# Selective-scan kernel: scans of places 1 and 2 over 513 columns, with hand-drawn waits on three PSUM banks

## The chip, the cores and the metric

The kernel runs on one core of one Trainium2 chip. The time is that of the device, in microseconds (us), from the start of the program on the core to its end; a result is the median of several executions. Five engines work side by side, each through its own queue in order: PE (matrix multiply), DVE (vector), ACT (scalar, with the activation functions), POOL (a second, slower vector engine) and SP (here it only issues DMAs). An instruction that waits holds up everything behind it on its engine.

## What is computed

A batch of 4 images of 128 channels and 128 x 128 points goes through two layers. The first, cut to what matters here, is a selective scan along the 16384 points of each image, for 256 inner channels with 16 states each:

```
delta = softplus(dt @ dt_proj_w.T + dt_proj_b)
A = -exp(A_log)
def step(h, inp):
    d_t, B_t, C_t, u_t = inp
    dA = exp(d_t[:, :, None] * A)
    h = h * dA + d_t[:, :, None] * B_t[:, None, :] * u_t[:, :, None]
    y = einsum('bds,bs->bd', h, C_t)
    return (h, y)
```

Around the scan stand small matrix products (an MLP, a projection, a convolution of 4 taps), a gate with silu(z), an output projection and a group norm. The second layer (group norm, an aggregation with softmax weights, and a filter in the Fourier domain) comes after it, partly between the chunks of later images.

## The kernel before, in words

**Chunks and units.** `block0` (from L148) cuts each image into 32 chunks of T = 512 points, 128 chunks k in all, and works on a chunk as 8 **units** U0 to U7 (u = 0..7: channel half j = u // 4, state group r = u % 4). A unit has 4 **places** p = 0..3; a place is 128 partitions (32 channels x 4 states) by 512 points. So a unit has four scans, one per place.

**One scan** is a `tensor_tensor_scan` on DVE (L412): state = da * state + b along the 512 points, where `da` = exp(delta * A) comes from ACT (L393) and b = du * B. It starts from the state that the same place had at the end of the chunk before: a column of a small tile `st`, given as an operand with one value per partition. Only in the first chunk of an image (k % 32 == 0) is the start the constant 0.0. For places 1 to 3, b is made by POOL in tile `hb` (L363, function `dbu`); for place 0 it is made by four PE transposes into the PSUM bank `b0` (L383, `dbu_turn`, here called the **turn**). `da` of place 0 lies in SBUF, those of places 1, 2 and 3 in one PSUM bank each.

**After a scan** the state is multiplied by C. For places 2 and 3 DVE does it (L414; the scan wrote in place over `da`), and ACT copies the last column to `st` (L415). For places 0 and 1 the scan writes to SBUF (`h`) and POOL multiplies both in one instruction of 1024 columns (L419); ACT copies the two last columns in the next slot (the **late** copy, printed under L554, the line that runs it). `by_vector` (L345) moves single places between the two: in odd chunks place 1 of U6 is multiplied by DVE too; in the chunks that also do the first group norm of the image before (k >= 32 and 2 <= k % 32 < 18, 48 chunks, here **norm chunks**) place 2 of U6 is done by POOL. `sums` (L422) adds the four products of a unit into the bank `y` with PE (L433); for U0 and U4 the bank is new, and a product with `diag` (L429) comes first, which must wait until the DVE gate (L443) has read the bank's old content.

**Order of the work.** Nothing is scheduled automatically: a list `todo` gives each piece a slot and a phase (L539 to L554), and the order in which pieces are emitted is the order on each engine. Each unit has an even slot (scans of places 0 and 1) and an odd slot (scans of places 2 and 3). Within a slot the phases run in the order of L551: turn, sums, pe, exps, late, act, pool, dbu, early, gate, scans, dve, end. What matters of it on ACT, before the change:

- even slot: `da` of places 2 and 3 of this unit, then the slot's other work (phases act and pool)
- odd slot: `da` of place 1 of the next unit, the late copy, the slot's other work, `da` of place 0 of the unit after the next (phase early), then the two copies of L415, which wait for the products on DVE

The other work of the 16 slots of a chunk: U1's even slot has silu of z and u (L242, L239), U3's has softplus (L275), each with two loads of an activation table around it; U3's odd slot copies `xdt` (L286); U4's and U5's odd slots start with, or contain, scalings `bt` of a transposed du (L304), which need PE transposes `pt_dut` (L293, `du_turn`) emitted in the pe phase of slots 8 and 11. Slot 11 is U5's odd slot. The gate of one half runs in slot 2 (U1), that of the other in slot 10 (U5). In 42 chunks (k % 32 >= 18 from k = 50 on, here **aggregation chunks**) the second layer's aggregation (L663, L667) and some transforms run in between too. The other 38 chunks that are not norm chunks are called plain.

Buffers: `hb` has 4, `h` 3, each PSUM bank of `b0` and `da` one. Which engine may touch a PSUM bank when is settled by the framework's waits, tile by tile.

Of the kernel before, what the change touches and what calls it, by code (L numbers as in the profile page):

```python
# [26 lines left out]
F32 = mybir.dt.float32  # L27
AF = mybir.ActivationFunctionType
ALU = mybir.AluOpType
# [4 lines left out]
P = 128  # L34
T = 512
DG = 32
SQ = 4
NP = 16
# [8 lines left out]
def kernel(ctx: ExitStack, tc: tile.TileContext, a: dict, out: bass.AP):  # L47
# [101 lines left out]
    spec = [dpool.tile([H, C, 2, WF], F32, tag=f"spec_{b}", name=f"spec_{b}") for b in range(EARLY)]  # L149
    shared = SimpleNamespace(**{k: v for k, v in locals().items() if k not in ("ctx", "tc")})  # L150
    block0(tc, shared)
    block1(tc, shared)


def block0(tc, s):
    nc, B, NCH, NH, NS, NG, ND, R, NX, KC, HALO, C, L, NF, DI = (
        s.nc, s.B, s.NCH, s.NH, s.NS, s.NG, s.ND, s.R, s.NX, s.KC, s.HALO, s.C, s.L, s.NF, s.DI,
    )
    NT = T // P
    with ExitStack() as ctx:  # L160
        def pool(name, bufs, **kw):
            return ctx.enter_context(tc.tile_pool(name=name, bufs=bufs, **kw))

        p1 = pool("p1", 1)
        p2 = pool("p2", 2)
        hpool = pool("hb", 4)
        tiny = pool("tiny", 2)
# [5 lines left out]
        psd = pool("psd", 1, space=PSUM)  # L173
# [4 lines left out]
        def turn_bank(n):  # L178
            return pst.tile([P, T], F32, tag="pt", name=f"pt_{n}")

        st = {}
        stats, outs = s.stats, s.outs

# [154 lines left out]
        def norming(k):  # L338

            return k >= NCH and 2 <= k % NCH < 2 + NCH // 2  # L340

        def place(r, p):


            return (p - r) % ND  # L345

        def by_vector(k, j, r, p):

            if norming(k):
                return p > 1 and (j, r, p) != (1, 2, 2)  # L350
            return p > 1 or (k % 2 == 1 and (j, r, p) == (1, 2, 1))

        def dbu(u):

            k, r = divmod(u, NH * NG)
            j, r = divmod(r, NG)
            d = st[k]
            hb = d["hb", j, r] = hpool.tile([P, ND, T], F32, tag="hb", name=f"hb_{k}_{j}_{r}")
            p = 1
            while p < NG:  # L360
                m = place(r, p)
                n = min(NG - p, ND - m)
                nc.gpsimd.tensor_tensor(  # L363
                    hb[:, p : p + n, :], d["du", j][:, m : m + n, :], d["B"][:, p - 1 : p - 1 + n, :], ALU.mult
                )
                p += n

        def pair(n):

            k, r = divmod(n, NP)  # L370
            u, p = divmod(r, ND // 2)
            j, r = divmod(u, NG)
            return k, j, r, 2 * p

        def dbu_turn(n):

            k, j, r, p = pair(n)
            d = st[k]
            if p == 0:
                b = d["b0"] = psd.tile([P, T], F32, tag="b0", name=f"b0_{k}_{j}_{r}")  # L380
                for t in range(NT):
                    src = d["bt"][:, t, j * ND + place(r, 0), :, :].rearrange("p s d -> p (s d)")
                    nc.tensor.transpose(b[:, t * P : (t + 1) * P], src, s.ident)  # L383

        def exps(n, qs):

            k, j, r, p = pair(n)
            d = st[k]
            for q in qs:
                m = place(r, p + q)  # L390
                c = (j * NG + p + q) * ND + m
                da = (psd if p + q else p2).tile([P, T], F32, tag=f"da{p + q}", name=f"da{p + q}_{k}_{j}_{r}")
                nc.scalar.activation(da, d["delta", j][:, m, :], AF.Exp, scale=s.amat[:, c : c + 1])  # L393
                d["da", j, r, p + q] = da

        def scans(n):


            k, j, r, p = pair(n)
            d = st[k]  # L400
            hb = d["hb", j, r]
            das = [d.pop(("da", j, r, p + q)) for q in range(2)]
            dve = [q for q in range(2) if by_vector(k, j, r, p + q)]
            pool = [q for q in range(2) if q not in dve]
            last = d["last", j, r, p] = tiny.tile([P, 2], F32, tag=f"st{j}_{r}_{p}", name=f"st_{k}_{j}_{r}_{p}")
            if pool:
                h = p2.tile([P, 2, T], F32, tag="h", name=f"h_{k}_{j}_{r}_{p}", bufs=3)
            for q in range(2):
                b = hb[:, p + q, :] if p + q else d.pop("b0")
                init = 0.0 if k % NCH == 0 else st[k - 1]["last", j, r, p][:, q : q + 1]  # L410
                o = das[q] if q in dve else h[:, q, :]
                nc.vector.tensor_tensor_scan(o, das[q], b, init, ALU.mult, ALU.add)  # L412
            for q in dve:
                nc.vector.tensor_tensor(hb[:, p + q, :], das[q], d["C"][:, p + q, :], ALU.mult)  # L414
                nc.scalar.copy(last[:, q : q + 1], das[q][:, T - 1 : T])  # L415
            if pool:
                q = slice(pool[0], pool[-1] + 1)
                ps = slice(p + pool[0], p + pool[-1] + 1)
                nc.gpsimd.tensor_tensor(hb[:, ps, :], h[:, q, :], d["C"][:, ps, :], ALU.mult)  # L419
                todo[n + 1, "late"].append(partial(nc.scalar.copy, last[:, q], h[:, q, T - 1]))  # L420

        def sums(u):  # L422

            k, r = divmod(u, NH * NG)
            j, r = divmod(r, NG)
            d = st[k]
            if r == 0:
                y = d["y", j] = psy.tile([P, T], F32, tag="y", name=f"y_{k}_{j}")
                nc.tensor.matmul(y, s.diag[:, j, :], d["u"][:, j, :], start=True, stop=False)  # L429
            y = d["y", j]  # L430
            for p in range(ND):
                m = place(r, p)
                nc.tensor.matmul(  # L433
                    y[m * DG : (m + 1) * DG, :], s.sel, d["hb", j, r][:, p, :], start=False, stop=r == NG - 1
                )

        def post(k):
# [66 lines left out]
        n_chunks = B * NCH  # L504
        todo = defaultdict(list)
# [33 lines left out]
        for n in range(n_chunks * NP):  # L539
            if n % 2 == 0:  # L540
                todo[n - 3, "early"].append(partial(exps, n, (0,)))
            todo[n - 1, "exps"].append(partial(exps, n, (1,) if n % 2 == 0 else (0, 1)))
            todo[n - 1, "turn"].append(partial(dbu_turn, n))
            todo[n, "scans"].append(partial(scans, n))
            if n % 2 == 0:
                todo[n - 2, "dbu"].append(partial(dbu, n // 2))
            else:
                todo[n + 2, "sums"].append(partial(sums, n // 2))
        slots = [n for n, _ in todo]
        with tc.manual_schedule():  # L550
            for n in range(min(slots), max(slots) + 1):  # L551
                for phase in ("turn", "sums", "pe", "exps", "late", "act", "pool", "dbu", "early", "gate", "scans", "dve", "end"):
                    for f in todo[n, phase]:
                        f()  # L554

# [500 lines left out]
```

## Time and profile before

| | us |
|---|---|
| median of 3 runs | 7172.46 (7171.05 to 7173.44) |
| the profiled execution, its own time | 7175.45 |
| its span | 7173.6 |
| main part with the scans (first to last scan) | 48.7 to 6407.5 |
| scans L412, place 0 and 1 to SBUF: x992, x1000 | 1258.3, 1251.6 |
| scans L412 in place, x1976 | 2419.8 |
| products L414 on DVE, x2040 | 1296.1 |
| products L419 on POOL, x1072 | 2435.0 |
| du * B on POOL, L363, x1536 | 3605.7 |
| exponentials on ACT, L393, x4096 | 2794.1 |

The times of the rows are sums over the whole span. Engines overlap, so the rows don't add up to the span: what counts is which engine has no idle time in a stage, and what a late result holds up there.

### The profile page before, as it was taken

What the parts mean: (1) busy time and instruction counts of PE and PEld (TensorE: products, weight loads), DVE (VectorE), ACT (ScalarE), POOL (GpSimd) and SP (SyncE); (2) the same over time, 40 slices, a digit from 0 to 9 for tenths busy, and PEclk for the clock granted to TensorE, in tenths of its full rate; (3) what the DMA queues carried; (4) which work ended last, traced back from release to release, by engine and by line L of the source; (5) the groups of instructions that cost most, each with busy time, mean ns of one, the idle gap of its engine ahead of it and who ended that gap; (6) DMA issues with size and microseconds to landing.
All of it is one profiled execution on the core that took longest, in us unless ns stands there. A gap on an engine that the chain in (4) does not pass through costs nothing.

```text
span 7173.6 us, 91384 instructions
## 1 busy us (share of the span) xinstructions
PE 5904.2 (82%) x26708; PEld 2626.8 (37%) x26708; DVE 6892.9 (96%) x7966; ACT 6143.9 (86%) x13658; POOL 6892.5 (96%) x3188
## 2 busy tenths in 40 slices
PE   6888888788787788888888788888887888867998
PEld 2333333233222233333333333333333333326888
DVE  6999999999999999999999999999999999989777
ACT  6888888888888888888888888898888888878876
POOL 6999999999999999999999999999999999988887
PEclk8888888888888889998989899999898899979999
DMA  5666666666777777777777777777777777769866
GB/s 139 160 160 152 163 159 151 165 159 165 191 176 192 179 171 176 172 184 175 189 196 186 188 176 175 178 177 184 189 191 194 177 179 177 172 164 306 236 185 162
DMA packets 905480, 1286.20 MB, mean 179 GB/s; under 512 B 81672, under 2 KB 356752, under 8 KB 904976
## 3 DMA queue, kind: packets, MB, share of 16 engines
q1 hardware_dynamic: 904832, 1280.09, 71.9%
q8 instruction: 210, 3.44, 0.2%
q14 instruction: 294, 2.41, 0.1%
q10 hardware_dynamic: 144, 0.26, 0.0%
HBM read 1023.45 MB, written 256.58 MB: 178 GB/s over the span
## 4 chain that ended last, share of the span: by engine, by line
DVE 41%; ACT 29%; issue 11%; PE 10%; DMA 5%; POOL 3%; SPq 1%; DVEq 0%; ACTq 0%; POOLq 0%
DVE da L412 20%; DVE h L412 12%; ACT da L393 12%; DVE hb L414 5%; ACT L393 3%; DMA rdelta<-dd 2%; ACT L275 2%; ACT delta L275 2%; ACT bt L304 2%; POOL hb L363 2%; DVE zs L443 1%; PE y L433 1%; POOL hb L419 1%; ACT L242 1%; DMA xt<-x 1%
## 5 line engine op out<-in xcount | busy, mean ns | idle before, releaser
L363 POOL TENSOR_TENSOR hb<-rdu,rB 128x1536 f32<-128x1536 f32 (+2 forms) x1536 | 3605.7, 2364 | 22.4 <-DMA rdelta<-dd 21.3
L393 ACT ACTIVATE da<-rdelta,amat 128x512 f32<-128x512 f32 x4096 | 2794.1, 700 | 138.3 <-DVE h L412 133.9
L419 POOL TENSOR_TENSOR hb<-h,rC 128x1024 f32<-128x1024 f32 (+1 forms) x1072 | 2435.0, 2274 | 88.8 <-DVE h L412 73.4
L412 DVE TENSOR_TENSOR_SCAN da<-da,st,hb 128x512 f32<-128x512 f32 x1976 | 2419.8, 1267 | 21.5 <-ACT da L393 14.3
L433 PE MATMUL y<-hb,sel 128*32 128x512 f32 x8192 | 1313.4, 717 | 2.9 <-POOL hb L419 2.7
L414 DVE TENSOR_TENSOR hb<-da,rC 128x512 f32<-128x512 f32 x2040 | 1296.1, 674 | 3.0
L412 DVE TENSOR_TENSOR_SCAN h<-da,st,b 128x512 f32<-128x512 f32 x992 | 1258.3, 1268 | 1.7 <-PE b L383 1.6
L412 DVE TENSOR_TENSOR_SCAN h<-da,st,hb 128x512 f32<-128x512 f32 x1000 | 1251.6, 1255 | 1.8 <-ACT da L393 1.8
L383 PE MATMUL b<-ident,bt 128*128 128x128 f32 x4096 | 748.4, 305 | 516.1 <-DVE h L412 390.6
L234 PE MATMUL pp_cv<-xm,wck 128*128 128x512 f32 x2048 | 1014.3, 640 | 1.6 <-ACT xm L217 0.8
L304 ACT ACTIVATE bt<-pt_dut,xdt 128x256 f32<-128x256 f32 x2048 | 839.4, 474 | 184.5 <-PE pt_dut L293 184.3
L383 PEld LDWEIGHTS b<-ident,bt 128*128 128x128 f32 x4096 | 531.3, 154 | 1017.1 <-DVE h L412 692.8
L415 ACT COPY st<-da 128x1 f32<-128x1 f32 x2040 | 273.1, 160 | 474.2 <-DVE hb L414 471.1
L234 PEld LDWEIGHTS pp_cv<-xm,wck 128*128 128x128 f32 x2048 | 395.9, 204 | 651.0 <-issue 422.1
L828 POOL TENSOR_TENSOR wb<-wb,term 128x1040 f32<-128x1040 f32 x192 | 461.0, 2401 | 70.8 <-ACT term L822 62.9
L293 PE MATMUL pt_dut<-ident,du 128*128 128x128 f32 x1024 | 232.4, 338 | 285.1 <-ACT xdt L286 174.9
L429 PE MATMUL y<-u,diag 128*128 128x512 f32 x512 | 303.0, 675 | 188.7 <-DVE zs L443 187.3
L293 PEld LDWEIGHTS pt_dut<-ident,du 128*128 128x128 f32 x1024 | 132.2, 162 | 604.8 <-POOL du L312 475.9
L393 ACT ACT_TABLE_LOAD x262 | 336.1, 1283 | 12.1 <-DMA rdelta<-dd 7.4
L312 POOL TENSOR_TENSOR du<-delta,u 128x512 f32<-128x512 f32 x256 | 318.8, 1267 | 25.8 <-ACT delta L275 25.8
L223 PE MATMUL pp_z<-xm,win 128*128 128x512 f32 x512 | 274.5, 634 | 51.8 <-ACT fq L497 46.2
L267 PE MATMUL pp_dt<-xd,wdt 8*128 8x512 f32 x512 | 284.8, 642 | 33.0 <-ACT pp_o L457 23.5
(160 smaller groups left out, 8139.8 us busy)
## 6 DMA issues: line engine op xcount, KB each, us to landing
rdelta<-dd SPq DMA_DIRECT2D x1024, 256.0 KB, 4.7
rdu<-dd SPq DMA_DIRECT2D x1024, 256.0 KB, 7.5
rC<-bc SPq DMA_DIRECT2D x512, 256.0 KB, 7.3
rB<-bc SPq DMA_DIRECT2D x512, 192.0 KB, 4.7
dd<-delta SPq DMA_DIRECT2D x256, 256.0 KB, 7.2
dd<-du SPq DMA_DIRECT2D x256, 256.0 KB, 5.7
ft<-in_filt_w SPq DMA_DIRECT2D x104, 520.0 KB, 7.0
ob<-o SPq DMA_DIRECT2D x128, 256.0 KB, 2.1
```

Of the source, the lines that this page charges most:

```text
L234: nc.tensor.matmul(ps["cv", j], w, d["xm"][:, t : t + T], start=t == 0, stop=t == KC - 1)
L293: nc.tensor.transpose(ps["dut"][:, 2 * t + j, :], d["du"][:, j, at : at + P], s.ident)
L304: nc.scalar.activation(d["bt"][:, 2 * h + t, :, q, :], src, AF.Copy, scale=d["xdt"][:, 2 * h + t, R + q : R + q + 1])
L312: nc.gpsimd.tensor_tensor(du, d["delta"][:, j, :], d["u"][:, j, :], ALU.mult)
L363: nc.gpsimd.tensor_tensor(hb[:, p : p + n, :], d["du", j][:, m : m + n, :], d["B"][:, p - 1 : p - 1 + n, :], ALU.mult)
L383: nc.tensor.transpose(b[:, t * P : (t + 1) * P], src, s.ident)
L393: nc.scalar.activation(da, d["delta", j][:, m, :], AF.Exp, scale=s.amat[:, c : c + 1])
L412: nc.vector.tensor_tensor_scan(o, das[q], b, init, ALU.mult, ALU.add)
L414: nc.vector.tensor_tensor(hb[:, p + q, :], das[q], d["C"][:, p + q, :], ALU.mult)
L419: nc.gpsimd.tensor_tensor(hb[:, ps, :], h[:, q, :], d["C"][:, ps, :], ALU.mult)
L433: nc.tensor.matmul(y[m * DG : (m + 1) * DG, :], s.sel, d["hb", j, r][:, p, :], start=False, stop=r == NG - 1)
L828: nc.gpsimd.tensor_tensor(wb, wb, u[n].terms[f], ALU.add)
```

## The change

The PSUM banks of `b0`, `da` 1 and `da` 2 become one tile `band` of three banks side by side. For a unit whose place 1 is multiplied by POOL (all but U6 of chunks that are not norm chunks), the scans of places 1 and 2 take 513 columns: the first is the last column of the bank to the left, with the constant start 0.0, and `hb` has a column more, whose value for places 1 and 2 is the old state. So 0.0 * a + b gives the old state, and the scan goes on from there. The old state gets there by an ACT copy of two columns (`carry`; in the first chunk of an image by a POOL memset). As the scans now read or write the last column of the neighbouring bank, the kernel draws the waits on the three banks itself (`on_band`): each user waits for the last users of its banks on the other engines, and no wait is drawn between users of different banks.

With it go: DVE multiplies place 1 of U6 in every chunk that is no norm chunk (before: odd ones); the order in an odd slot is place 3, then 2, for scans, products and copies, and ACT makes `da` 3 before `da` 2; `da` 1 of the next unit is emitted inside `scans` of the odd slot, after the scan of place 2 and so behind the early `da` 0; the turn comes after sums; and `hb` and `h` have rows of 513 columns, of which the products and sums use the last 512.

```diff
+        band = psd.tile([P, 3 * T], F32, tag="band", name="band")
+        users = []
+        def on_band(engine, banks, made):
+            i = made.ins
+            seen = set()
+            for e, b, j in reversed(users):
+                if e == engine:
+                    continue
+                if not b & banks:
+                    tc.declare_no_dep(i, j, reason="another bank")
+                    continue
+                for bank in b & banks:
+                    if (e, bank) not in seen:
+                        seen.add((e, bank))
+                        tc.add_manual_dep(
+                            i, j.name, mybir.DependencyInfo(mybir.DependencyClass.Sync, mybir.DependencyReason.DATA),
+                            reason="same bank",
+                        )
+            users.append((engine, banks, i))
+            del users[:-40]
...
-            return p > 1 or (k % 2 == 1 and (j, r, p) == (1, 2, 1))
+            return p > 1 or (j, r, p) == (1, 2, 1)
...
-            hb = d["hb", j, r] = hpool.tile([P, ND, T], F32, tag="hb", name=f"hb_{k}_{j}_{r}")
+            hb = d["hb", j, r] = hpool.tile([P, ND, 1 + T], F32, tag="hb", name=f"hb_{k}_{j}_{r}")
...
+        def carried(k, j, r):
+            return () if by_vector(k, j, r, 1) else (1, 2)
+        def carry(u):
+            k, r = divmod(u, NH * NG)
+            j, r = divmod(r, NG)
+            if carried(k, j, r):
+                o = st[k]["hb", j, r][:, 1:3, 0]
+                if k % NCH == 0:
+                    nc.gpsimd.memset(o, 0.0)
+                else:
+                    nc.scalar.copy(o, st[k - 1]["last", j, r][:, 1:3])
...
+                if p + q in (1, 2):
+                    da = band[:, (p + q) * T : (p + q + 1) * T]
...
-                h = p2.tile([P, 2, T], F32, tag="h", name=f"h_{k}_{j}_{r}_{p}", bufs=3)
+                h = p2.tile([P, 2, 1 + T], F32, tag="h", name=f"h_{k}_{j}_{r}_{p}", bufs=3)
+            order = (1, 0) if p else (0, 1)
+            for q in order:
+                if p + q in carried(k, j, r):
+                    a = band[:, (p + q) * T - 1 : (p + q + 1) * T]
+                    o = a if q in dve else h[:, q, :]
+                    made = nc.vector.tensor_tensor_scan(o, a, hb[:, p + q, :], 0.0, ALU.mult, ALU.add)
+                    on_band("DVE", {p + q - 1, p + q}, made)
+                    continue
...
+            if p and n + 1 < n_chunks * NP:
+                exps(n + 1, (1,))
+            for q in [q for q in order if q in dve]:
...
-            todo[n - 1, "exps"].append(partial(exps, n, (1,) if n % 2 == 0 else (0, 1)))
+            if n % 2 or n == 0:
+                todo[n - 1, "exps"].append(partial(exps, n, (1, 0) if n % 2 else (1,)))
...
+                todo[n - 1, "carry"].append(partial(carry, n // 2))
...
-                for phase in ("turn", "sums", "pe", "exps", "late", "act", "pool", "dbu", "early", "gate", "scans", "dve", "end"):
+                for phase in ("sums", "turn", "pe", "exps", "late", "carry", "act", "pool", "dbu", "early", "gate", "scans", "dve", "end"):
```

More of the change, by code (lines that the diff above doesn't have):

```diff
@@ L363, in dbu @@
                 nc.gpsimd.tensor_tensor(
-                    hb[:, p : p + n, :], d["du", j][:, m : m + n, :], d["B"][:, p - 1 : p - 1 + n, :], ALU.mult
+                    hb[:, p : p + n, 1:], d["du", j][:, m : m + n, :], d["B"][:, p - 1 : p - 1 + n, :], ALU.mult
                 )
                 p += n
+        def carried(k, j, r):
[9 more added lines that the diff above has]
+                    nc.scalar.copy(o, st[k - 1]["last", j, r][:, 1:3])
         def pair(n):
@@ L379, in dbu_turn @@
             if p == 0:
-                b = d["b0"] = psd.tile([P, T], F32, tag="b0", name=f"b0_{k}_{j}_{r}")
+                b = band[:, 0:T]
                 for t in range(NT):
                     src = d["bt"][:, t, j * ND + place(r, 0), :, :].rearrange("p s d -> p (s d)")
-                    nc.tensor.transpose(b[:, t * P : (t + 1) * P], src, s.ident)
+                    on_band("PE", {0}, nc.tensor.transpose(b[:, t * P : (t + 1) * P], src, s.ident))
         def exps(n, qs):
@@ L391, in exps @@
                 c = (j * NG + p + q) * ND + m
-                da = (psd if p + q else p2).tile([P, T], F32, tag=f"da{p + q}", name=f"da{p + q}_{k}_{j}_{r}")
-                nc.scalar.activation(da, d["delta", j][:, m, :], AF.Exp, scale=s.amat[:, c : c + 1])
+                if p + q in (1, 2):
+                    da = band[:, (p + q) * T : (p + q + 1) * T]
+                else:
+                    da = (psd if p else p2).tile([P, T], F32, tag=f"da{p + q}", name=f"da{p + q}_{k}_{j}_{r}")
+                made = nc.scalar.activation(da, d["delta", j][:, m, :], AF.Exp, scale=s.amat[:, c : c + 1])
+                if p + q in (1, 2):
+                    on_band("ACT", {p + q}, made)
                 d["da", j, r, p + q] = da
@@ L404, in scans @@
             pool = [q for q in range(2) if q not in dve]
-            last = d["last", j, r, p] = tiny.tile([P, 2], F32, tag=f"st{j}_{r}_{p}", name=f"st_{k}_{j}_{r}_{p}")
+            if p == 0:
+                d["last", j, r] = tiny.tile([P, ND], F32, tag=f"st{j}_{r}", name=f"st_{k}_{j}_{r}")
+            last = d["last", j, r][:, p : p + 2]
             if pool:
-                h = p2.tile([P, 2, T], F32, tag="h", name=f"h_{k}_{j}_{r}_{p}", bufs=3)
[L408 to L412, printed above, removed]
@@ L413, in scans @@
-            for q in dve:
-                nc.vector.tensor_tensor(hb[:, p + q, :], das[q], d["C"][:, p + q, :], ALU.mult)
-                nc.scalar.copy(last[:, q : q + 1], das[q][:, T - 1 : T])
+                h = p2.tile([P, 2, 1 + T], F32, tag="h", name=f"h_{k}_{j}_{r}_{p}", bufs=3)
[7 more added lines that the diff above has]
+                    continue
+                b = hb[:, p + q, 1:] if p + q else band[:, 0:T]
+                init = 0.0 if k % NCH == 0 else st[k - 1]["last", j, r][:, p + q : p + q + 1]
+                o = das[q] if q in dve else h[:, q, 1:]
+                made = nc.vector.tensor_tensor_scan(o, das[q], b, init, ALU.mult, ALU.add)
+                if p + q < 3:
+                    on_band("DVE", {p + q}, made)
@@ new lines, in scans @@
+            if p and n + 1 < n_chunks * NP:
+                exps(n + 1, (1,))
+            for q in [q for q in order if q in dve]:
+                made = [
+                    ("DVE", nc.vector.tensor_tensor(hb[:, p + q, 1:], das[q], d["C"][:, p + q, :], ALU.mult)),
+                    ("ACT", nc.scalar.copy(last[:, q : q + 1], das[q][:, T - 1 : T])),
+                ]
+                if p + q < 3:
+                    for engine, i in made:
+                        on_band(engine, {p + q}, i)
@@ L418, in scans @@
                 ps = slice(p + pool[0], p + pool[-1] + 1)
-                nc.gpsimd.tensor_tensor(hb[:, ps, :], h[:, q, :], d["C"][:, ps, :], ALU.mult)
-                todo[n + 1, "late"].append(partial(nc.scalar.copy, last[:, q], h[:, q, T - 1]))
+                nc.gpsimd.tensor_tensor(hb[:, ps, 1:], h[:, q, 1:], d["C"][:, ps, :], ALU.mult)
+                todo[n + 1, "late"].append(partial(nc.scalar.copy, last[:, q], h[:, q, T]))
         def sums(u):
@@ L433, in sums @@
                 nc.tensor.matmul(
-                    y[m * DG : (m + 1) * DG, :], s.sel, d["hb", j, r][:, p, :], start=False, stop=r == NG - 1
+                    y[m * DG : (m + 1) * DG, :], s.sel, d["hb", j, r][:, p, 1:], start=False, stop=r == NG - 1
                 )
```

## The prediction

> **What bounds the kernel now.** I read the page's busy shares first, then stretches of one chunk each, then the groups kept apart by form, then the order of time on single engines. The shares leave DVE and POOL level:
>
> ```profile
> PE 5904.2 (82%) x26708; PEld 2626.8 (37%) x26708; DVE 6892.9 (96%) x7966; ACT 6143.9 (86%) x13658; POOL 6892.5 (96%) x3188
> ```
>
> The stretches are an even plain chunk, an odd one and a norm chunk (busy us of PE, PEld, DVE, ACT, POOL):
>
> ```profile
> 458.25:506.62 48.37, 40.45 (x157) 15.10 (x156) 48.37 (x51) 41.70 (x93) 47.50 (x22) 0.90 0.67 159
> 506.62:555.73 49.11, 38.49 (x150) 13.80 (x150) 49.08 (x52) 42.02 (x94) 49.11 (x24) 0.87 0.66 157
> 1978.49:2028.78 50.29, 40.20 (x156) 14.60 (x155) 50.26 (x54) 43.23 (x95) 50.06 (x24) 0.92 0.75 184
> ```
>
> DVE has no idle time in any of them: it is the bound. POOL has 0.87 us of slack in two plain chunks together, 0.23 in a norm chunk. ACT idles 7 us a chunk, but its queue is in order, so what counts is when each exponential lands.
>
> **What the constant start saves.** Rows by form:
>
> ```profile
> L412 DVE TENSOR_TENSOR_SCAN da<-da,st,hb 128x512 f32<-128x512 f32 x1976 | 2419.8, 1267 | 21.5 <-ACT da L393 14.3 <-POOL hb L363 3.6 <-issue 3.4
> ...
> L412 DVE TENSOR_TENSOR_SCAN da<-da,hb 128x512 f32<-128x512 f32 x64 | 74.5, 1209 | 1.4 <-issue 1.4
> ...
> L412 DVE TENSOR_TENSOR_SCAN h<-da,hb 128x512 f32<-128x512 f32 x32 | 38.3, 1197 | 3.8 <-POOL hb L363 3.5 <-ACT da L393 0.2
> ```
>
> With a column as start a scan takes 1.267 (1.255 to SBUF, place 1), from the constant 1.209 and 1.197. Starts show the same step: 1.174 becomes 1.114, 60 ns. The 513th column costs at most 1.2 us / 512 = 2 ns, so 58 ns a scan, on DVE, the bound. A plain chunk has 7 such units, 14 scans, 0.81 us; a norm chunk 16 scans, 0.93. Bounds: crossing a bank edge is in no row; the saving could be nothing.
>
> **What it moves.** U6's place 1 on DVE in every plain chunk: the odd chunk is 0.74 longer than the even one, so the mean 48.74 becomes 49.11 - 0.81 = 48.30 before new waits. POOL gives up one 512-column product (2363 - 1276 ns = 1.09 us) in even chunks: (47.50 + 49.11 - 1.09) / 2 = 47.8, so DVE stays the bound. A norm chunk: DVE 50.29 - 0.93 = 49.36; POOL's 50.06 becomes its floor, 0.23 won at most. Rows of 513 columns on POOL: L899 writes 8 rows apart, 520 columns in 1298 ns, where the line through 512 (1276) and 1024 columns (2363) gives 1293, so I take 0. The far bound is a whole instruction's fixed part, 0.19 us (1276 - 1087), for each extra row.
>
> [...]
>
> `carry` adds 944 ACT or POOL writes of two columns; the late copy, the same shape, steps 0.08 us (519.45 to 519.54). It does not wait for POOL's `hb` beside it: at 7159.71 ACT (L905) writes other columns of a tile that POOL (L900) is still writing.
>
> **Where the new waits land.** On ACT `da` of place 1 now stands behind the late copy, carry, the slot's other work and the early `da` 0. Before, it came first. U1 of a plain chunk (scan of place 0 at 512.52):
>
> ```profile
> 517.53 1.28 ACT L393 ACT_TABLE_LOAD   x1
> 518.83 0.69 ACT L393 ACTIVATE da<-rdelta,amat 128x512 f32<-128x512 f32 x1
> 519.45 0.18 ACT L554 COPY st<-h 128x2 f32<-128x2 f32 x1
> 519.54 0.72 ACT L393 ACTIVATE da<-rdelta,amat 128x512 f32<-128x512 f32 x1
> ```
>
> Times from the unit's start: `da` 1 ends at 7.00. After: two copies 0.16 and `da` 0 (step 0.62) first, so 7.78. A place-1 scan that waited started 0.10 after its `da` (1718.91 + 0.69, scan at 1719.70), so 7.88. U2's place-1 scan stood at 520.20, 7.68; with two scans 58 ns shorter it is due at 7.56. **A wait of 0.32.** U3 (start 524.91; softplus): `da` 1 ended 530.97, 6.06; plus 0.16, xdt 0.18, 0.62, 0.10 = 7.12; due 531.99 - 524.91 - 0.12 = 6.96. **0.16.** U5 (start 536.70) is worse, since ACT's L304 there waits for PE, and PE now does sums, held by the gate, before the turn:
>
> ```profile
> 542.52 0.47 ACT L304 ACTIVATE bt<-pt_dut,xdt 128x256 f32<-128x256 f32 x1 [1.28 <-PE pt_dut L293]
> 542.89 0.71 ACT L393 ACTIVATE da<-rdelta,amat 128x512 f32<-128x512 f32 x1
> ```
>
> ```profile
> 538.02 0.66 PE L383 MATMUL b<-ident,bt 128*128 128x128 f32 x4
> 539.78 1.12 PE L429 MATMUL y<-u,diag 128*128 128x512 f32 x2 [1.10 <-DVE zs L443]
> 540.83 1.07 PE L433 MATMUL y<-hb,sel 128*32 128x512 f32 x8
> 541.83 0.66 PE L293 MATMUL pt_dut<-ident,du 128*128 128x128 f32 x4
> ```
>
> The turn's four transposes (step 0.49, as 541.83 to 542.32) move between 541.83 and L293: bt at 5.82 + 0.49 - 0.06 (an earlier gate) = 6.25, `da` 0 at 6.62, `da` 1 at 7.24, end 7.93, scan 8.03, due 544.38 - 536.70 - 0.12 = 7.56. **0.47.** The turn itself ends at 5.6, before U6's first scan at 6.38. Together 0.95 a plain chunk; a norm chunk has U1's wait hidden (two norm additions and two statistics on DVE there), so 0.63. With the scan starting 0.03 after its `da`, as other scans do, it would be 0.74. DVE was the bound, so each wait is whole time, until POOL is.
>
> **PE's clock.** With the turn gone from there, PE stands still from L199's end to the gate. In an aggregation chunk before (k = 90):
>
> ```profile
> 4548.84 0.59 PE L199 MATMUL pp_h<-xt,w 128*128 128x512 f32 x1
> 4551.27 0.66 PE L383 MATMUL b<-ident,bt 128*128 128x128 f32 x4 [1.84 <-DVE h L412]
> 4553.02 1.83 PE L429 MATMUL y<-u,diag 128*128 128x512 f32 x2 [1.10 <-DVE zs L443]
> 4554.78 1.94 PE L433 MATMUL y<-hb,sel 128*32 128x512 f32 x8
> 4556.65 0.67 PE L293 MATMUL pt_dut<-ident,du 128*128 128x128 f32 x4
> ```
>
> L429 to L293 takes 3.63 instead of 2.05: half clock after the two gaps. This happens in 15 of 42 such chunks. The gap becomes one of 3.5 us, so I take nearly all: 1.58 us later, up to 2.04 with a turn at half clock (526.23, 1.12 instead of 0.66); I take 1.6, since the clock may fall only during the run; lower bound 0. In plain and norm chunks the gap is some 1.7 (538.05 to 539.78): 0.3, between 0 and 2.04. All of it lands on U5's wait.
>
> [...]
>
> **The sum,** in us, against the profiled execution's 7175.45 (span 7173.6; 3.0 over the runs' median 7172.46, to which I add it):
>
> - 34 plain chunks: 48.30 + 0.95 + 0.3 = 49.55 against 48.74: +27.5
> - 42 aggregation chunks: 48.30 + 0.95 + 0.1 (two activations more in U4) + 1.6 = 50.95 against 48.98 (2533.77 to 3220.12 in 14, 4129.07 to 4813.95 in 14): +83
> - 4 first chunks, which started from the constant already: 0.74 + 0.95 + 0.3: +8
> - 48 norm chunks: 49.36 + 0.63 + 0.3 = 50.29 against 50.29: 0
>
> +118, so about **7290 us**.
>
> A change within 0.2% (14 us) is about what a measurement of this kernel can't tell from none.
>
> **Rivals.**
>
> *The waits hide, and it is faster:* `da` 1 lands in time. For: ACT idles 7 us a chunk; against: the three rows above. 76 chunks x -0.44, 4 x +0.74, 48 x -0.23 = -41: 7131. The point at which it turns: waits of 0.44 us a plain chunk. Chance 0.20; 0.10 more that half the waits hide and it is within 0.2%.
>
> *The waits, and PE stays warm:* for: in 27 of 42 aggregation chunks L429 ran at full clock; against: the gap grows. 34 x 0.51 + 42 x 0.37 + 4 x 1.69 - 48 x 0.23 = +29: 7201. Chance 0.22.
>
> *POOL slows on rows apart:* 12 rows more in du * B and 8 in products at 0.19 us are 3.9 us a chunk: 80 x (51.7 - 48.8) + 48 x (54.0 - 50.3) = some +400, 7580. L899 speaks against. It decides from 1.7 us, POOL's slack then. Chance 0.05.
>
> *The scans don't get shorter* (bank edge, start one column off): 1832 scans x 58 ns = 106 more, 7395; against: nothing but the constant's rows. Chance 0.05.
>
> *As forecast:* 0.38, from 7225 (clock loss a third) to 7340 (2.04 in aggregation chunks, 0.6 elsewhere).
>
> Faster 0.20, the same 0.10, slower 0.70. The range leaves out the last two rivals: 7128 to 7340.
>
> **What would show it.** Scans of place 1 and 2 at about 1.21; waits of DVE for ACT's `da` at U2, U4 and U6, place 1, of 0.3, 0.2 and 0.5 us; L429 at half clock in most aggregation chunks; POOL's products still 2.36; a plain chunk of 49.2 to 49.6. It would be wrong if DVE still ran without idle time in a plain chunk, or if a wait stood at another place, such as the turn, or carry behind POOL.

## The result, and the profile after

The changed kernel takes 7329.09 us (median of 4 runs, 7328.66 to 7330.66), the one before 7171.76 (7169.87 to 7173.44): a ratio of 1.022, 95% interval 1.0202 to 1.0238. It is slower, by 157 us; the forecast was 118 more than the 7172.46 measured ahead of it, so 7290. The profiled execution of the changed kernel took 7328.99, its span 7327.2.

First the shares. The page's busy line of the changed kernel:

```profile
PE 5913.0 (81%) x26708; PEld 2620.1 (36%) x26708; DVE 6855.3 (94%) x8006; ACT 6232.5 (85%) x14614; POOL 6701.9 (91%) x3216
```

DVE has 37 us less work than before, but the span is 154 longer: DVE waits now. POOL has 191 us less. Three chunks as stretches (plain, k = 9; aggregation, k = 54; norm, k = 41; busy us of PE, PEld, DVE, ACT, POOL, then PE's granted clock):

```profile
519.13:569.46 50.33, 38.83 (x153) 13.62 (x153) 48.58 (x53) 42.61 (x101) 46.70 (x23) 0.93 0.66 153
2784.83:2838.13 53.30, 43.22 (x177) 16.46 (x176) 48.79 (x52) 44.55 (x107) 46.70 (x23) 0.90 0.67 161
2124.30:2174.26 49.96, 38.70 (x153) 13.98 (x152) 49.43 (x54) 43.94 (x105) 48.76 (x24) 0.93 0.73 186
```

Subtract DVE's busy time from the length: idle 1.75 us in the plain chunk, 4.5 in this aggregation chunk (one of the longest), 0.5 in the norm chunk. Before, it was at most 0.04 at the median of each of these three classes. Averaged from the starts of the first scans, the chunks went from 49.08 to 50.34 (34 plain), from 48.99 to 51.61 (aggregation), from 47.13 to 49.45 (first chunks, without that of the first image, which holds the start) and from 50.53 to 50.38 (48 norm). 34 x 1.26 + 42 x 2.62 + 4 x 2.3 - 48 x 0.15 = 155: the whole difference of the profiled spans lies there, and some 70% of it in the aggregation chunks.

The scans and POOL's products, rows by form:

```profile
L457 DVE TENSOR_TENSOR_SCAN band<-band,hb 128x513 f32<-128x513 f32 x896 | 1081.7, 1207 | 0.0
```

```profile
L479 POOL TENSOR_TENSOR hb<-h,rC 128x1024 f32<-128x1024 f32 x944 | 2066.3, 2189 | 410.5 <-DVE h L457 397.8 <-DVE rstd L661 5.5 <-DVE total L756 1.9
```

The scans of place 2 over 513 columns across a bank edge take 1.207 us, where they took 1.267, and those of place 1 to SBUF take 1.207 as well, where they took 1.255: the saving is there. POOL's product fell from 2.363 to 2.189, which nobody had foreseen.

DVE's waits, by the last releaser (us, times, longest), first two of the kernel before, then three of the changed one:

```profile
DVE h L412 <- PE b L383: 40.0, 4, 38.4
DVE h L412 <- ACT da L393: 2.1, 4, 0.7
```

```profile
DVE h L463 <- PE band L420: 113.7, 86, 40.8
DVE h L457 <- ACT st L471: 61.9, 138, 3.1
DVE band L463 <- ACT st L471: 61.5, 78, 1.3
```

The first line of the changed kernel is place 0 waiting for the turn: 40.8 of it is one wait at the start of the program, as before; nearly all of the other 73 is new. The second and third are place 1, the third being U6's, which is in place. They name ACT's two small copies, but look at the order on ACT below: the copies are issued just after `da` 1 and overlap its end, so they come last in the profile while `da` 1 is what the scan needs (in experiment 2 the profile names `da` 1 itself).

Now one aggregation chunk where it is lost (k = 54, U5 starts at 2815.95), PE and then ACT in order of time:

```profile
2813.41 1.98 PE L221 MATMUL pp_h<-xt,w 128*128 128x512 f32 x4
2819.27 2.05 PE L489 MATMUL y<-u,diag 128*128 128x512 f32 x2 [3.88 <-DVE zs L503]
2821.25 1.94 PE L493 MATMUL y<-hb,sel 128*32 128x512 f32 x8
2823.12 1.12 PE L420 MATMUL band<-ident,bt 128*128 128x128 f32 x4
```

```profile
2825.12 0.47 ACT L326 ACTIVATE bt<-pt_dut,xdt 128x256 f32<-128x256 f32 x1 [4.12 <-PE pt_dut L315]
...
2826.10 0.68 ACT L433 ACTIVATE band<-rdelta,amat 128x512 f32<-128x512 f32 x1
2826.71 0.15 ACT L471 COPY st<-da 128x1 f32<-128x1 f32 x1
```

PE stands still for 3.88 us, and after that the products take up to twice as long (the turn 1.12 instead of 0.66), at a granted clock of 0.51 from 2819.2 to 2825.0. The turn ends 8.3 us after U5's start, where U6's first scan was due at 6.4; `bt` comes at 9.2, `da` 0 and `da` 1 behind it, and the scan of place 1 at 10.9. One stall on PE delays DVE twice.

### The profile page after: what moved, and what is told of

Its sections match the earlier page's. It is cut to its first block, busy times and chain, and to the rows that moved or that the text cites. A ratio compares the mean times of both kernels' runs of the same rounds, so it can differ in the third digit from the quotient of the medians.

```text
span 7327.2 us, 94364 instructions
## 1 busy us (share of the span) xinstructions
PE 5913.0 (81%) x26708; PEld 2620.1 (36%) x26708; DVE 6855.3 (94%) x8006; ACT 6232.5 (85%) x14614; POOL 6701.9 (91%) x3216
## 3 DMA queue, kind: packets, MB, share of 16 engines
q8 instruction: 211, 3.46, 0.2%
## 5 line engine op out<-in xcount | busy, mean ns | idle before, releaser
L385 POOL TENSOR_TENSOR hb<-rdu,rB 128x1536 f32<-128x1536 f32 (+2 forms) x1536 | 3607.2, 2364 | 43.1 <-DMA rdelta<-dd 20.8
L433 ACT ACTIVATE band<-rdelta,amat 128x512 f32<-128x512 f32 x2048 | 1402.8, 685 | 219.5 <-DVE band L457 219.2
L433 ACT ACTIVATE da<-rdelta,amat 128x512 f32<-128x512 f32 x2048 | 1458.8, 712 | 4.0 <-ACT st L471 0.2
L463 DVE TENSOR_TENSOR_SCAN h<-da,st,band 128x512 f32<-128x512 f32 x992 | 1262.8, 1273 | 71.8 <-PE band L420 71.1
L457 DVE TENSOR_TENSOR_SCAN h<-band,hb 128x513 f32<-128x513 f32 x992 | 1197.8, 1207 | 83.6 <-ACT st L471 61.9
L463 DVE TENSOR_TENSOR_SCAN da<-da,st,hb 128x512 f32<-128x512 f32 x992 | 1262.1, 1272 | 2.3 <-ACT da L433 1.9
L457 DVE TENSOR_TENSOR_SCAN band<-band,hb 128x513 f32<-128x513 f32 x896 | 1081.7, 1207 | 0.0
L420 PEld LDWEIGHTS band<-ident,bt 128*128 128x128 f32 x4096 | 500.5, 158 | 1218.3 <-DVE h L457 573.9
L420 PE MATMUL band<-ident,bt 128*128 128x128 f32 x4096 | 780.5, 320 | 181.5 <-DVE h L457 156.3
L470 DVE TENSOR_TENSOR hb<-band,rC 128x512 f32<-128x512 f32 x1056 | 716.7, 679 | 2.7
L470 DVE TENSOR_TENSOR hb<-da,rC 128x512 f32<-128x512 f32 x1024 | 689.4, 673 | 0.0
```

The source lines that it names most:

```text
L385: nc.gpsimd.tensor_tensor(hb[:, p : p + n, 1:], d["du", j][:, m : m + n, :], d["B"][:, p - 1 : p - 1 + n, :], ALU.mult)
L420: on_band("PE", {0}, nc.tensor.transpose(b[:, t * P : (t + 1) * P], src, s.ident))
L433: made = nc.scalar.activation(da, d["delta", j][:, m, :], AF.Exp, scale=s.amat[:, c : c + 1])
L457: made = nc.vector.tensor_tensor_scan(o, a, hb[:, p + q, :], 0.0, ALU.mult, ALU.add)
L463: made = nc.vector.tensor_tensor_scan(o, das[q], b, init, ALU.mult, ALU.add)
L470: ("DVE", nc.vector.tensor_tensor(hb[:, p + q, 1:], das[q], d["C"][:, p + q, :], ALU.mult)),
```

## The experiments

Times are medians of several runs, and line numbers in an experiment's rows are its own; the kernel before, on the same chip, took 7172.5 to 7175.1. "Slow" counts chunks in which `diag` to the end of sums took over 2.9 us (2.1 at full clock), and chunk lengths are worked out from the starts of scans; the last chunk of the aggregation class has no following start, so 41 are counted. Idle times at a place are means over all chunks of the class, 42 in that of the aggregation.

**1. The turn first again** (7239.34 us, 1.0092, interval 1.0077 to 1.0107).

```diff
-                for phase in ("sums", "turn", "pe", "exps", "late", "carry", "act", "pool", "dbu", "early", "gate", "scans", "dve", "end"):
+                for phase in ("turn", "sums", "pe", "exps", "late", "carry", "act", "pool", "dbu", "early", "gate", "scans", "dve", "end"):
```

> The changed kernel with the turn ahead of sums again, as the kernel before had it; everything else as changed. Theory (two causes: da 1 late on ACT, and a turn behind sums that the gate holds and that then run at half clock): the second cause goes, so DVE's waits at U2 and U6 place 0 (0.54 a plain chunk, 0.90 an aggregation chunk) vanish, bt comes again some 5.8 us into U5, and the wait at U6 place 1 falls to 0.1 or less. The waits at U2 and U4 place 1 stay at 0.3 and 0.2. Plain chunk 48.85, aggregation chunk 48.95: about 7160 us. Rival (ACT's order alone makes the loss): 7290 or more. Rival (the turn now waits for the scan of place 1, so that sums and all behind them come late in every unit): no better than 7329.

90 us of the 157 go, not 170. DVE's waits for the turn go entirely (43.1 us left in 4 waits, 41.3 of them the start), and U1's sums are at full clock in all chunks counted. But in aggregation chunks U6 place 1 still waits 1.11, and U5's sums are slow in 33 of 41: the turn now waits for the scan of place 1, so PE still stands still for 2.2 us ahead of it. The theory holds for the turn; that the clock would recover with it was wrong.

**2. da 0 behind da 1** (7256.84 us, 1.0119, interval 1.0102 to 1.0136).

```diff
             if p and n + 1 < n_chunks * NP:
                 exps(n + 1, (1,))
+            if p and n + 3 < n_chunks * NP:
+                exps(n + 3, (0,))
...
-            if n % 2 == 0:
+            if n in (0, 2):
                 todo[n - 3, "early"].append(partial(exps, n, (0,)))
```

> The changed kernel with da 0 (the early one, of the unit after the next) moved behind da 1 of the next unit on ACT; the turn stays behind sums. Theory: da 1 comes 0.62 us earlier, so that the waits at place 1 of U2, U4 and U6 in plain chunks (0.12, 0.32, 0.42) go, and of 1.09 at U6 in aggregation chunks some 0.5 is left; the waits at place 0 for the turn stay (0.54 and 0.90). About 34 x 0.8 + 42 x 1.1 = 75 us less than 7329: 7255. Rival (the copies and the work of the slot are what delays da 1, or da 1 waits for DVE's scan of place 2): less than 20 us won. Rival (ACT's order is the only cause): below 7172.

The sum is as expected (7255), its parts are not. The waits at place 1 fall to 0.1 (U4), 0.2 (U6 plain) and 0.4 (U6 aggregation), and those at place 0 stay (0.41 at U2 plain, 0.98 at U6 aggregation). The aggregation chunks win 1.1 each, as expected. But the plain chunks win nothing (50.33): U5's sums are slow there in 14 of 34 instead of none, and the wait at U6 place 0 grew from 0.04 to 0.50. The norm chunks win 0.46 that wasn't counted. The order on ACT is a cause by itself, of about 70 us; on PE it leaves the clock as it was or worse.

**3. Both** (7138.54 us, 0.995, interval 0.9935 to 0.9964).

> Both edits together: the turn ahead of sums and da 0 behind da 1. Theory: all new waits go, and what is left is the shorter scans: DVE without idle time in plain and aggregation chunks at 48.3 to 48.4 us, norm chunks at POOL's floor of 50.1. 34 x -0.8 + 42 x -0.6 + 48 x -0.4 + 3 against 7175: 7105 to 7135 us, faster than both kernels. Rival (waits are merely traded for others, at POOL or at U2's table loads): 7150 to 7172.

Faster than both kernels. The stretch of k = 54 again, that took 53.30:

```profile
2721.72:2770.45 48.73, 41.42 (x180) 16.40 (x180) 48.47 (x52) 44.24 (x108) 47.09 (x23) 0.96 0.72 175
```

DVE is within 0.26 us of full, and k = 9 takes the same 48.73. Together the edits win 191 us, more than 90 + 72: each cause fed the other. With `da` 1 early the scan of place 1 in U5, and so the turn, comes sooner; PE's gap in aggregation chunks is 1.97 us on average instead of 2.22, and U5's sums are slow in 5 of 41 chunks instead of 33. The time is 4 us above the expected range.

**4. The start from the column again, all else as changed** (7438.60 us, 1.0368, interval 1.0352 to 1.0383).

```diff
-            return () if by_vector(k, j, r, 1) else (1, 2)
+            return ()
```

> The changed kernel with all scans started from the column of the state again: no scan has 513 columns and no carry is made; order, band and waits as changed. Theory (a start from the constant saves 58 ns a scan): scans of places 1 and 2 take 1.25 to 1.27 us again, DVE is busy 106 us more; where ACT's da 1 is late anyway, the longer scans of the unit before fill the wait (0.12 for each such wait), so that some 50 to 90 us of it show: 7380 to 7420. Rival (the 513 columns over the bank edge, or carry, cost as much as the constant saves): 7320 to 7340.

110 us more than the changed kernel: the saving is real. Of it, 96 us are DVE's busy time (6951.0 instead of 6855.3), the rest is idle time. That waits would swallow part of the saving was wrong. The waits grew: those for the turn from 113.7 to 154.8 us, those named for ACT's copies from 123.4 to 110.3 only. With the longer scans PE's gap in U1 of the aggregation chunks got longer (2.34 us on average instead of 1.98), and U1's sums were slow there in 17 of 41 chunks instead of 4.

**5. PE kept at work in the gap, too much** (7383.81 us, 1.029, interval 1.0273 to 1.0308). In aggregation chunks the h1 product is computed 9 times over instead of once.

```diff
+                    for _ in range(9 if j and k >= 52 and (k - 2) % NCH >= 18 else 1):
                         nc.tensor.matmul(ps["h", j], s.w1[:, j * P : (j + 1) * P], d["xt"], start=True, stop=True)
```

> The changed kernel, in aggregation chunks alone with 8 more products on PE just behind the h1 product at the end of U4 (the same product again into the same bank, so that the values stay), 0.43 us each: PE works through the gap before the gate of U5. The order of all else is as changed, the turn behind sums too. Theory (half clock after the gap of 3.9 us makes the aggregation chunks' loss): diag and sums take 2.1 us instead of 3.2, the turn comes in time for U6 (wait of 0.90 at place 0 gone), bt at 6.25 instead of about 9, the wait at U6 place 1 falls from 1.09 to 0.5; 42 x -1.5 = 63 us less than 7329: 7265. Plain and norm chunks as in the changed kernel. Rival (the place of the turn in PE's order makes it, whatever the clock): 7325 or more.

Mis-sized: one product is two matmuls of 0.43, so 8 are 6.9 us, and `diag` came at 6.1 us into U5 instead of 3.3. Only this is left of it: with no gap ahead, `diag` to the end of sums took 2.06 us on average (slow in 1 of 41).

**6. PE kept at work in the gap, 4 products** (7260.08 us, 1.0123, interval 1.0107 to 1.0138). As before, with 5 instead of 9.

> The changed kernel, in aggregation chunks alone with 4 more products on PE behind the h1 product (the same product again into the same bank): each is two matmuls of 0.43 us, so 3.4 us in a gap of 3.9. With 8 of them (6.9 us) the gate's products came 2.8 us late, but took 2.06 us instead of 3.2. Theory (PE's half clock after the gap makes most of the loss in these chunks): diag starts as before at 3.3 us into U5 and takes 2.1; the turn is in time for U6 (wait of 0.90 at place 0 gone), and the wait at U6 place 1 falls from 1.09 to 0.5; 42 x -1.5 = 63 us less than 7329: 7265. Rival (the turn's place in PE's order makes it, whatever the clock): 7320 or more.

69 us less than the changed kernel. The order of work is the same, and PE even does more; the gap alone is filled. PE in the same place (k = 54, U5 starts at 2805.81):

```profile
2803.26 5.42 PE L222 MATMUL pp_h<-xt,w 128*128 128x512 f32 x12
2809.12 1.10 PE L490 MATMUL y<-u,diag 128*128 128x512 f32 x2 [0.44 <-DVE zs L504]
...
2811.15 0.66 PE L421 MATMUL band<-ident,bt 128*128 128x128 f32 x4
```

The wait at U6 place 0 fell from 0.90 to 0.07, that at place 1 from 1.09 to 0.38. An aggregation chunk fell from 51.61 to 50.17 us, 1.44 of the 2.62 that it had lost: so the clock by itself, with the turn's place in the queue unchanged, makes more than half of the loss there. Of the 71 us between the two profiled spans, 53 lie in the main part with the scans; 4 lie ahead of it and 14 behind it, and why stays open.

**7. The kernel before with sums first** (7245.48 us, 1.0101, interval 1.0086 to 1.0116).

```diff
-                for phase in ("turn", "sums", "pe", "exps", "late", "act", "pool", "dbu", "early", "gate", "scans", "dve", "end"):
+                for phase in ("sums", "turn", "pe", "exps", "late", "act", "pool", "dbu", "early", "gate", "scans", "dve", "end"):
```

> The kernel before with one edit, sums ahead of the turn; scans, da and the waits as before. Theory: this edit alone makes the loss of PE's clock. DVE waits for the turn at U2 place 0 in plain chunks (0.5) and at U6 place 0 in aggregation chunks (0.9, and some more for a late bt), and for nothing at place 1, since da 1 comes early there: 34 x 0.5 + 42 x 1.1 = 63 more, about 7235. Rival (with da 1 early the order on PE is harmless): within 10 us of 7172.

This one edit, without a new scan or wait, costs the kernel before 70 us. DVE's idle time at U6 place 0 is 1.14 in aggregation chunks and nothing at place 1; U5's sums are slow in 38 of 41 (23 in the kernel before). In plain chunks it was less than expected, 0.16 at U2 and at U6 each.

**8. Both, without the 513 columns** (7242.77 us, 1.0096, interval 1.0081 to 1.0111). Experiment 3 with the edit of experiment 4.

> The kernel with both edits (turn first, da 0 behind da 1) and all scans started from the column again, without carry. Theory: with the waits gone DVE is the bound in all chunks, so the whole of 1832 scans x 58 ns = 106 us is seen against the 7138 of the kernel with both edits, less what waits at U6 and at table loads take up: 7225 to 7245. That is above the 7172 of the kernel before, because POOL gives one product of U6 to DVE in the even chunks (40 x 0.74 = 30) and the self-wait at U6 (80 x 0.2 = 16) remain. Rival (the gain of the kernel with both edits came from the order, not from the shorter scans): 7150 or less.

104 us more than experiment 3. Not all of that is scan time: U6 place 1 waits 0.68 in aggregation chunks here (0.21 in experiment 3), some 20 us; a plain chunk takes 49.36 against 48.73 at the median, 0.63 for 14 scans, with 0.12 of small idle times at U2 and U4, place 3, that only experiment 3 has.

**9. U6 place 1 to SBUF** (7276.73 us, 1.0149, interval 1.0134 to 1.0164). Experiment 3, and:

```diff
-            return () if by_vector(k, j, r, 1) else (1, 2)
+            return (1, 2)
...
-                    o = a if q in dve else h[:, q, :]
+                    o = a if p and q in dve else h[:, q, :]
...
+                out = das[q] if p else h[:, q, 1:]
                 made = [
-                    ("DVE", nc.vector.tensor_tensor(hb[:, p + q, 1:], das[q], d["C"][:, p + q, :], ALU.mult)),
-                    ("ACT", nc.scalar.copy(last[:, q : q + 1], das[q][:, T - 1 : T])),
+                    ("DVE", nc.vector.tensor_tensor(hb[:, p + q, 1:], out, d["C"][:, p + q, :], ALU.mult)),
+                    ("ACT", nc.scalar.copy(last[:, q : q + 1], out[:, T - 1 : T])),
                 ]
-                if p + q < 3:
+                if p and p + q < 3:
```

> The kernel with both edits (turn first, da 0 behind da 1), and in U6 the scan of place 1, that wrote in place over its bank, writes to SBUF like the other place-1 scans; so U6 also starts places 1 and 2 from the carried column in all chunks. What is left of idle time in plain and aggregation chunks there is a step of 1.40 us from the scan of place 0 to that of place 1 of U6, where the other units take 1.19, with a wait of DVE on its own last scan in between. Theory: that wait goes (0.21) and two scans are 58 ns shorter (0.12): 80 x 0.33 = 26 us less than 7138: 7112. Rival (the scan there waits for ACT's copies, that come just before): 9 us less at most.

The scan did what was expected: its step fell from 1.40 to 1.19. But the kernel lost 138 us. The products on DVE, rows by form:

```profile
L473 DVE TENSOR_TENSOR hb<-band,rC 128x512 f32<-128x512 f32 x976 | 663.3, 680 | 0.0
L473 DVE TENSOR_TENSOR hb<-h,rC 128x512 f32<-128x512 f32 x80 | 209.6, 2620 | 2.8
```

The same product takes 0.68 us from PSUM and 2.62 from SBUF: 80 x 1.94 = 155 us, more than the 138 lost; how much of the expected 26 the scans won back can't be told apart. One of the 80, DVE and then POOL:

```profile
154.34 1.20 DVE L457 TENSOR_TENSOR_SCAN h<-band,hb 128x513 f32<-128x513 f32 x1
155.58 6.72 DVE L473 TENSOR_TENSOR hb<-h,rC 128x512 f32<-128x512 f32 x1
162.22 1.28 DVE L463 TENSOR_TENSOR_SCAN da<-da,st,hb 128x512 f32<-128x512 f32 x1
```

```profile
153.52 3.63 POOL L385 TENSOR_TENSOR hb<-rdu,rB 128x1024 f32<-128x1024 f32 x2
157.07 1.31 POOL L482 TENSOR_TENSOR hb<-h,rC 128x512 f32<-128x512 f32 x1
158.29 3.46 POOL L385 TENSOR_TENSOR hb<-rdu,rB 128x1536 f32<-128x1536 f32 x1
```

The product ends at 162.3, 0.55 us after POOL's last instruction there (158.29 + 3.46); 0.68 is what it needs. All 80 end so, 0.51 to 0.55 us after the end of a POOL instruction; 32 took under 0.9 us, the others up to 6.74. So the end of this product goes with the end of a POOL instruction. Which POOL instruction that is, when POOL issues one after another, is not settled by the rows: in those shown the product lasted through four POOL instructions, while the 32 short products ran between two that followed without a pause. Why they go together was not shown.

**10. That product on POOL** (7064.72 us, 0.9847, interval 0.9832 to 0.9861). Experiment 3, and:

```diff
-            return p > 1 or (j, r, p) == (1, 2, 1)
+            return p > 1
```

> The kernel with both edits, and POOL takes the product of place 1 of U6 in every chunk. POOL's products of 1024 columns take 2.19 us in all kernels with rows of 513, where they took 2.36 before, so POOL has 7 x 0.17 = 1.2 us more slack a chunk, and the product costs it 0.91. Theory: as DVE is the bound, its 0.6 for that product goes, and with it the 0.21 and 0.12 at U6: 80 x 0.93 = 74 us less than 7138: 7064. Rival (POOL becomes the bound, at 47.2 busy and its waits): 7090 to 7140.

7064 was expected. It is the fastest kernel here, 110 us below the one before on the same chip (7175.08). The plain stretch (k = 9):

```profile
499.11:546.74 47.63, 39.55 (x153) 14.31 (x153) 47.54 (x51) 42.27 (x102) 47.42 (x23) 0.89 0.66 163
```

DVE and POOL are level again, at 47.5 us; in an odd chunk before it was 49.1.

**11. The kernel before with rows of h 513 apart** (7179.65 us, 1.0009, interval 1.0 to 1.0019).

```diff
-                h = p2.tile([P, 2, T], F32, tag="h", name=f"h_{k}_{j}_{r}_{p}", bufs=3)
+                h = p2.tile([P, 2, 1 + T], F32, tag="h", name=f"h_{k}_{j}_{r}_{p}", bufs=3)
...
-                o = das[q] if q in dve else h[:, q, :]
+                o = das[q] if q in dve else h[:, q, 1:]
...
-                nc.gpsimd.tensor_tensor(hb[:, ps, :], h[:, q, :], d["C"][:, ps, :], ALU.mult)
-                todo[n + 1, "late"].append(partial(nc.scalar.copy, last[:, q], h[:, q, T - 1]))
+                nc.gpsimd.tensor_tensor(hb[:, ps, :], h[:, q, 1:], d["C"][:, ps, :], ALU.mult)
+                todo[n + 1, "late"].append(partial(nc.scalar.copy, last[:, q], h[:, q, T]))
```

> The kernel before with the rows of h, that POOL's products of places 0 and 1 read, 513 columns apart instead of 512, and nothing else. All kernels with such rows (of h and of hb) run these products in 2.19 us instead of 2.36. Theory (it is h, as du * B into rows of 513 takes 2.36 as before): the products of 1024 columns take 2.19 us and those of 512 columns 1.28 as before; DVE is the bound, so the time stays within 10 us of 7172. Rival (the rows of hb make it): 2.36. Rival (POOL also bounds the chunks with DVE): 7150 or less.

POOL's products of this kernel, where nothing but `h` is changed:

```profile
L419 POOL TENSOR_TENSOR hb<-h,rC 128x1024 f32<-128x1024 f32 x984 | 2152.1, 2187 | 258.6 <-DVE h L412 255.4 <-DVE total L694 1.7 <-DVE pooled L671 0.4
```

2.187 us, so it is the rows of the input `h`. It is not that they start a column later: the products of one row of 512, which start there too, took 1.277 us, and 1.276 before. The edit wins POOL 173 us and the kernel nothing, since POOL only waits longer for DVE. Why two rows apart are read faster than one row of 1024 stays open.

## Why the prediction was right, and where it was not

The direction and the mechanism were right, the size was 39 us short (118 against 157).

**The saving** (58 ns a scan): right. 1.207 us was measured for 513 columns across a bank edge, in place and to SBUF; from the constant, 512 columns in one bank took 1.209 in place, which was taken, and 1.197 to SBUF: the edge costs 0.01 at most. Taken away, it costs 110 us in the changed kernel, against 106 worked out; the match is close in part by luck, as some 14 of the 110 are idle time that grew.

**The waits for `da` 1** (0.95 a plain chunk): right in kind and size. DVE's idle time at place 1 of U2, U4 and U6 was 0.12, 0.32 and 0.42, and each such wait also loses about 0.08 of overlap between scans (in U0 of k = 9 of the kernel before, the scan of place 0 took 1.27 and the next began 1.19 after its start): 1.1. In U5 of k = 9 even the instants fit: `bt` at 6.27 (6.25 predicted), the scan at 8.02 (8.03). Two details are worth a look. U4 waits 0.32 instead of 0.16, since ACT was already late there behind a copy of the output projection, which comes later on PE (in U2 of k = 9 ACT stood 1.04 us for it). And at U6 the prediction knew only ACT's lateness, which explains the whole wait here (in k = 9 `da` 1 ended at 558.11 and the scan began at 558.20); but behind it hides a wait of DVE on its own semaphore, for its own last scan. It shows where `da` 1 is in time: a step of 1.40 instead of 1.19 at the median of the plain chunks in experiments 1, 3 and 8. It goes with the in-place scan on `band` and is gone in experiments 9 and 10.

**PE's clock in plain chunks** (0.3, all on U5's wait): the wrong place. U5's sums were never slow in plain chunks of the changed kernel, U1's in 20 of 34, each time after a single gap of 2.36 us. PE in U1 of k = 9, whose next unit should have begun at 531.3:

```profile
528.02 2.04 PE L489 MATMUL y<-u,diag 128*128 128x512 f32 x2 [2.36 <-DVE zs L503]
530.00 1.63 PE L493 MATMUL y<-hb,sel 128*32 128x512 f32 x8
531.55 0.66 PE L420 MATMUL band<-ident,bt 128*128 128x128 f32 x4
```

Here the turn itself is late, and U2's first scan waits 0.88 (0.54 on average). The step that failed is the sentence that the turn "ends at 5.6, before U6's first scan at 6.38": it was worked out at full clock only, beside a term that assumed half clock, and for U5 only. At half clock the turn ended at 7.3 to 8.3. This is most of the plain chunks' 0.45 us excess, 15 of the missing 39 us.

**PE's clock in aggregation chunks** (1.6): right in mechanism, as experiment 6 shows; all 41 were slower than 2.3 us from `diag` to the end of sums, 39 of them slow. The 1.6 and 0.47 for U6 add up to 2.07; measured were 0.90 at place 0 and 1.09 at place 1, and the lost overlap; the prediction had put all of it on place 1. What was left out is U2 (0.39 idle and two lost overlaps against 0.32 taken), U4 (0.25 against 0.16) and U5 (0.09). Also, by the count used here the kernel before was slow in 23 of 41, not in 15 of 42; the loss from it was smaller because only `bt` came late there, not the turn. The excess is 0.65 a chunk, 27 us. Of the 42 us that the two classes took beyond the sum, 7 are hidden by what the norm chunks won.

In the traces of the kernels before and after, the granted clock changes only at multiples of 3.41 us. These are three such windows around U1's sums of k = 9 in the changed kernel (busy us of PE, PEld, DVE, ACT, POOL, then PE's granted clock):

```profile
524.36:527.77 3.41, 1.30 (x4) 0.23 (x2) 3.41 (x5) 2.93 (x7) 3.36 (x3) 1.00 0.65 135
527.77:531.18 3.41, 3.16 (x10) 0.70 (x10) 3.41 (x5) 3.41 (x6) 3.41 (x2) 0.50 0.00 0
531.18:534.59 3.41, 3.41 (x14) 1.17 (x11) 2.53 (x4) 3.40 (x8) 1.92 (x2) 1.00 0.02 5
```

PE was busy for 0.38 of the first, and the second was granted half clock. All 20 slow chunks have such a window ahead, 0.31 to 0.38 busy; in the 14 others the least busy one was 0.42 to 0.62. So here a gap counted by where it fell on this grid, and not by its length alone: two of the 14 had the same gap of 2.36 us. A sharp threshold is not shown: in U5 of the aggregation chunks of the kernel before the clock fell after windows up to 0.48 busy, and windows from 0.46 on passed without a fall; in experiments 1 and 3 it fell up to 0.49, and windows from 0.43 on passed. In these two 33 of 41 chunks were slow with a mean gap of 2.22 us, and 5 of 41 with 1.97.

**Norm chunks** (no change): won 0.15 instead. The step that failed is POOL's "floor" of 50.06. POOL's products became faster, its work in the norm chunk shown is 48.76, and DVE bounds there too; in experiments 3 and 10 these chunks run at 49.2 to 49.3 at the median.

**POOL's rows of 513** (cost 0): du * B agreed (2.364 before, 2.364 after), the products were off on the other side, 0.17 us faster each.

**The rivals.** "The waits hide" at 7131 lies near the kernel with both edits, 7138.54, but by luck. That rival had 33 us won in plain and aggregation chunks and 11 in norm chunks. In experiment 3 the plain and aggregation chunks stand at 49.13 and 48.94, within 0.05 of the kernel before, and the norm chunks fell from 50.53 to 49.72, which is 39 us: POOL's "floor" was gone. What a plain chunk saves in scans, 0.81, went into U6's place 1 on DVE (0.37, as forecast) and into idle time and lost overlap at U6, U2 and U4. The order on two queues spent 191 us on top. "PE stays warm" at 7201 was tried in part: with PE at work ahead of U5 in aggregation chunks alone the time is 7260, where the forecast less 42 x 1.6 gives 7223. "The scans don't get shorter" and "POOL slows" are out by the rows above.

## What to carry to other kernels

When an edit moves work on an in-order queue behind something that waits, add up not only the queue's delay, but also the gap that it opens on that engine, and work out every follower of the gap at the slow clock too (here `diag` and sums took 3.2 us instead of 2.1). Two late results on two queues can feed each other: try the cures one by one and together, as here 90 and 72 us became 191. A change that is right in its core can lose by the order of what surrounds it; before it is dropped, put each moved phase back by itself.

## What the runs showed of the hardware

- In experiment 9 a product on DVE with both inputs in SBUF took 0.69 to 6.74 us beside a busy POOL, and all 80 ended 0.51 to 0.55 us after a POOL instruction; with one input in PSUM it took 0.68.
- In the kernel before and in experiment 11, POOL's product of 1024 columns took 2.363 us when the input `h` was one row of 1024, and 2.187 when it was two rows of 512, 513 apart. The output's rows had no such effect in du * B (2.364 in the kernel before, 2.364 in the changed one).
- A scan from the constant over 513 columns across a PSUM bank edge took 1.207 us in the changed kernel, one over 512 columns in one bank 1.209 in place and 1.197 to SBUF in the kernel before.
- PE's granted clock changed only at multiples of 3.41 us in the traces of the kernels before and after. Around U1's sums of the changed kernel's plain chunks it fell after windows in which PE was busy for 0.31 to 0.38, and not after windows of 0.42 and more. `diag` and sums, 2.1 us at full clock, took 3.2 on average in U5 of the aggregation chunks.
